# A routed-expert kernel: routing weights by tangent, one scan per chunk, the eight-largest instructions in small chunks, and filling rows in the first batch

## The chip, the cores and the metric

The kernel runs on one core of a Trainium2 chip. The metric is the device time of one execution in microseconds (us). The runs shown for the kernel before are 1497.51, 1497.18 and 1500.99 us, with a median of 1497.51. A profiled execution was recorded beside them. Of the engines, PE multiplies matrices, DVE works on vectors, ACT evaluates activation functions, POOL does general work and issues indirect DMAs (gathers and scatters by row numbers), and SP issues the plain DMAs. Each engine works through its own instructions in their order and waits on semaphores for the others.

## The reference, cut to what matters

The input x has 64 graphs ("batches") of 256 nodes with 256 features. Two layers follow one another; each is an attention over the graph's edges and then a feed-forward part, both added to x:

```python
x = x + gnn0(layernorm(x), adj)          # 4 heads, softmax over neighbours, elu
x = x + layernorm(x) @ weight.T + bias
x = x + gnn1(layernorm(x), adj)          # 1 head, softmax over neighbours, relu
x = x + moe(layernorm(x))                # below
```

The last part sends each row ("token") to two of eight experts:

```python
logits = tokens @ router_w.T
probs = softmax(logits)
rw, re = top_k(probs, 2)
rw = rw / max(rw.sum(-1), 1e-12)
combine = zeros(N, 8).at[row, re].set(rw)
out = tokens
for e in range(8):
    h = gelu(tokens @ w1[e] + b1[e])
    out = out + combine[:, e] * (h @ w2[e] + b2[e])
```

With the two largest logits a >= b, the two weights of a row depend on b - a alone: the first is 1 / (1 + exp(b - a)), the second 1 minus the first. Their difference is tanh((a - b) / 2).

## The kernel before, in words

**Batches and steps.** The program is written out by a loop in Python, which runs in steps; three steps (TICKS) begin one batch. In every step the active jobs (generators) are advanced in the order of their ranks, so each engine's order of instructions is fixed when the program is built. The job of a batch (`batch_layers`) does both attentions and the first feed-forward part on 256 rows, with everything in fp32. The inverse root for the norms runs on POOL (L408, L409, L446, L449, tile `rstd`), and at the end of the program on DVE. A batch ends with its normalized rows (`xng`), its logits (`lg`) and the rows `base` = x + layernorm(x), which SP stores into the output (L736).

**Chunks and routing.** CHUNKS is `(4,) * 11 + (2,) * 7 + (1,) * 3`: the first 61 batches are routed in 21 chunks of four, two or one batches. With NT = 2 tiles of 128 rows for each batch, a chunk has nt = 8, 4 or 2 tiles. `route` finds the two largest logits and their experts (`top_two`, L785 to L808), counts rows for each expert by two matmuls against ones (L1105, L1106), turns the counts into row places by a running sum over the tiles, expert by expert (L1116 in one instruction where nt is 8, otherwise one for each expert, L1122), takes the exponential of b - a on ACT (L1112), makes the two weights of it on DVE (`two_weights`, L812 to L815), and sends each row, with its own number and the two weights, to the region of each of its experts in a DRAM buffer `xs` (POOL's indirect DMAs, L1061). `allot` decides which pairs of tiles (256 rows of one expert) are full.

**Expert pairs.** `expert_pair` loads one pair (`xr`, L893) and its small columns (`xt`, L904) and the expert's first matrix (`we`, L922) on SP, multiplies twice on PE (`ph` L955, then `py` L970) with a Gelu on ACT between (`hT`, L961), adds the bias on DVE (`y`, L980), scales on ACT (L948), and puts the result into a list, from which one pair is taken in each step. `scatter` then adds the pair's 256 rows to the output by two indirect DMAs on POOL with addition (L991). Since two pairs may hold the same row, each pair's adds wait for the two adds before them:

```python
before = added[-2:] + based
```

**Filling rows.** A pair that isn't full at the end is filled with rows of the tile `fill`: zeros, weight 0, and as row number a row of the last batch, 63. They are added like all others, and add zero. So the last batch's rows are set to zero in setup (`fill_spare`, a 256 KB store on SP), and the last batch's own rows may be stored only when every add has landed.

**Dense batches.** The last three batches aren't routed. `route_dense` makes a weight for each row and expert (with an exponential, L1195, and `two_weights`), and `dense_expert` runs all eight experts on all their rows, adding into `base` on DVE (L1023). `store_dense` stores `base` on SP (L1036). For the last batch it holds the store back and then waits for the last adds:

```python
while b == B - 1 and (scatters or len(added) < 2 * PAIRS):
    yield 99
```

**Activation tables.** [...] the build puts a load (ACT_TABLE_LOAD) ahead of an activation whose function isn't in the set that is active. The kernel uses Exp (L479, L513, L647, L1112, L1195), Gelu (L961), and Square, Relu, Copy and Identity.

Of the kernel before, what the change touches and what calls it, by code (L numbers as in the profile page):

```python
# [15 lines left out]
P = 128  # L16
# [11 lines left out]
def kernel(  # L28
# [251 lines left out]
    def pack_expert(e):  # L280
# [22 lines left out]
    fill = const.tile([P, 2, ROW], F32, tag="fill", name="fill")  # L303
    nc.gpsimd.memset(fill, 0.0)
    nc.gpsimd.iota(
        fill[:, :, D : D + 1].bitcast(I32), pattern=[[1, 2], [1, 1]], base=(B - 1) * N,
        channel_multiplier=2,
    )
    nc.vector.memset(fill[:, :, D + 1 : D + 2], -1.0)
# [3 lines left out]
    def fill_spare():  # L313
        nc.sync.dma_start(
            out=xs_d[E * CAP * PAIR :, :].rearrange("(p t) c -> p t c", t=2), in_=fill
        )
        d = nc.sync.dma_start(
            out=out_rows[(B - 1) * N :, :].rearrange("(p t) c -> p t c", t=2), in_=fill[:, :, :D]
        )
        tc.add_to_no_dep_group("out", d.ins)  # L320
        based.append(d.ins)
        yield 90

    def once(work):
# [27 lines left out]
    em8 = iota([E], [[1, E]], -E, 0, "em8")  # L352
    jrow = iota([JOBS], [[1, JOBS]], 0, 0, "jrow")
    region = iota([E], [[CAP, E]], 0, 0, "region")
    scan_mask = const.tile([P, E, NTC], F32, tag="scan_mask", name="scan_mask")
    nc.vector.memset(scan_mask, 1.0)
    nc.vector.memset(scan_mask[:, :, 0:1], 0.0)

# [414 lines left out]
    def chunk_tile(shape, name, c, bufs=2, dt=F32):  # L773
        return keep.tile([P] + shape, dt, tag=name, name=f"{name}_{c}", bufs=bufs)
# [8 lines left out]
    def top_two(c, nt, lg, first):  # L783


        rt = lambda shape, name: chunk_tile(shape, name, c)
        vec, tt = nc.vector, nc.vector.tensor_tensor
        emb = em8[:, None, :].to_broadcast([P, nt, E])
        ohs, tops, lcur = rt([2, nt, E], "ohs"), [], lg
        for k in range(2):  # L790
            top = rt([nt], f"top{k}")
            vec.tensor_reduce(top, lcur, AX.X, ALU.max)
            eq = rt([nt, E], "eq")
            tt(eq, lcur, top[:, :, None].to_broadcast([P, nt, E]), ALU.is_equal)
# [12 lines left out]
        tt(ed, tops[1], tops[0], ALU.subtract)  # L807
        yield ohs, ed  # L808

    def two_weights(less, second, ed):  # L810

        nc.vector.tensor_scalar(less, ed, 1.0, None, op0=ALU.add)  # L812
        nc.vector.reciprocal(less, less)
        nc.vector.tensor_tensor(second, ed, less, ALU.mult)
        nc.vector.tensor_tensor(less, less, second, ALU.subtract)  # L815

    rows = [keep.tile([P, E], F32, tag="rows", name="rows")]  # L820
    nc.vector.tensor_scalar(rows[0], region, float(PAIR), None, op0=ALU.mult)
# [208 lines left out]
    def store_dense(b):  # L1030

        own = dense_batch[b]
        yield 99
        while b == B - 1 and (scatters or len(added) < 2 * PAIRS):
            yield 99
        d = nc.sync.dma_start(  # L1036
            out=out_rows[b * N : (b + 1) * N, :].rearrange("(t p) d -> p t d", p=P),
            in_=own["base"],
        )
        before = added[-2:] + based if b == B - 1 else []  # L1040
        tc.declare_no_dep(
            d.ins, query=SYNC, group="out", keep=before,
            reason="no row is added to here, or every add is in their chain",
        )
        for ins in before:
            tc.add_manual_dep(d.ins, ins.name, AFTER, reason="filling rows were added here")
        tc.add_to_no_dep_group("out", d.ins)
        nc.sync.nop()

# [29 lines left out]
    def route(c, row0, nt, n, last, xng, lg):  # L1079
# [32 lines left out]
        nc.scalar.activation(ed, ed, AF.Exp)  # L1112
        tt(tot[:, :, 0], tot[:, :, 0], rows[0], ALU.add)
        run = rt([E, nt], "run")
        if nt == NTC:
            vec.tensor_tensor_scan(  # L1116
                run.rearrange("p e t -> p (e t)"), scan_mask.rearrange("p e t -> p (e t)"),
                tot.rearrange("p e t -> p (e t)"), 0.0, ALU.mult, ALU.add,
            )
        else:  # L1120
            for e in range(E):
                vec.tensor_tensor_scan(  # L1122
                    run[:, e, :], ones[:, :nt], tot[:, e, :], 0.0, ALU.mult, ALU.add
                )
        rows[0] = run[:, :, nt - 1]
        tt(pre, pre, run, ALU.add)
        if spread:
# [8 lines left out]
        vec.tensor_copy(pos, posf)  # L1136
        if not spread:
            yield from later(90, 1, 2)
        two_weights(tail[:, :, 1], tail[:, :, 2], ed)
        for i, xe in enumerate(xng):  # L1140
            vec.tensor_copy(xe[:, :, D + 1 :], tail[:, i * NT : (i + 1) * NT, :])
        parts = allot(c, n, False)
# [47 lines left out]
    def route_dense(b, lg):  # L1190
# [4 lines left out]
        nc.scalar.activation(ed, ed, AF.Exp)  # L1195
        two = chunk_tile([2, NT], "two", c)
        two_weights(two[:, 0], two[:, 1], ed)
        nc.vector.tensor_tensor(two[:, 0], two[:, 0], two[:, 1], ALU.add)
        w = chunk_tile([NT, E], "wd", c, DENSE)
        nc.vector.tensor_tensor(  # L1200
# [8 lines left out]
                )  # L1209

    FLUSH = 2 * (E - 1)
    PAIRS = ROUTED * NT + E - 1

    def jobs():
        b = done = taken = 0
# [104 lines left out]
```

## Time and profile before

| | |
|---|---|
| median of three runs | 1497.51 us (1497.18 to 1500.99) |
| profiled execution, its own time | 1509.41 us |
| span, first to last instruction | 1507.6 us |
| mean granted PE clock | 0.986 |
| instructions | 30029 |
| table loads on ACT: in front of L961, L513, L1112, L647, L1195, L235 | 65, 47, 8, 6, 3, 1; 1283 ns each |
| indirect DMAs: adds into the output (L991), sends to the regions (L1061) | 258 and 244 |

The profile is one execution on the chip. "Busy" is the time in which an engine works on an instruction, as a share of the span. "Idle before, releaser" is the time that an engine waited ahead of an instruction, and whose semaphore came last. In the table by stage a row gives the stretch, its length, the busy time (and count) of PE, PEld (the loading of PE's weights), DVE, ACT and POOL, the granted PE clock, the share of DMA engines that were busy and GB/s. The profiled execution is 0.8% longer than the median of the runs, and its time is 1.8 us more than its span.

### The profile page before, as it was taken

The numbers are of one execution on the slowest core, as the hardware profiler recorded it, in microseconds if no ns is written. First come the engines' busy times: TensorE is split into PE (matmuls) and PEld (weight loads), VectorE is DVE, ScalarE is ACT, GpSimd is POOL, SyncE is SP. The second block draws the span as 40 slices with busy tenths as digits, with TensorE's granted clock in tenths as the row PEclk, the third lists the DMA queues.
The fourth block names the chain that finished last, engine by engine and source line by source line (L and its number), as shares of the span: only waits on it lengthen the run. The fifth ranks groups of instructions, "written<-read, shape, count | busy, mean of one in ns | idle before, by whom it ended". The sixth has DMA issues, their size and how long they took to land. (4 is left out here: it accounts for less than half of the span.)

```text
span 1507.6 us, 30029 instructions
## 1 busy us (share of the span) xinstructions
PE 1429.0 (95%) x8138; PEld 1263.9 (84%) x8138; DVE 1252.7 (83%) x4476; ACT 1024.6 (68%) x2403; POOL 870.2 (58%) x845
## 2 busy tenths in 40 slices
PE   6899999999999999999999999999999999879996
PEld 5788888889898998988998989888888887658885
DVE  7699999888898888889898988998888888765543
ACT  1477667577777777777777787667777878764331
POOL 2122536355867576666758585776666667643444
PEclk9899999899999999999999999999999999999999
DMA  4732334556877777877877677768777775887843
GB/s 134 241 97 67 117 104 131 155 149 142 196 172 190 157 183 155 177 177 180 187 157 183 151 186 164 181 164 187 179 167 170 153 170 124 192 180 161 156 83 50
DMA packets 354354, 236.37 MB, mean 157 GB/s; under 512 B 246276, under 2 KB 316428, under 8 KB 354188
## 3 DMA queue, kind: packets, MB, share of 16 engines
q1 hardware_dynamic: 301272, 158.16, 41.3%
q0 software_dynamic: 48864, 66.33, 23.8%
q10 hardware_dynamic: 4052, 9.98, 2.2%
q8 instruction: 67, 1.10, 0.3%
q14 instruction: 99, 0.81, 0.2%
HBM read 146.00 MB, written 88.35 MB: 155 GB/s over the span
## 5 line engine op out<-in xcount | busy, mean ns | idle before, releaser
L991 POOL DMA_INDIRECT out_dram<-y,xt x258 | 414.1, 1605 | 206.6 <-issue 71.5
L586 PE MATMUL pv<-q,z 128*128 128x65 f32 (+1 forms) x2560 | 365.9, 298 | 0.4
L586 PEld LDWEIGHTS pv<-q,z 128*128 128x128 f32 x2560 | 333.0, 194 | 13.1 <-DVE z L572 1.1
L1061 POOL DMA_INDIRECT xs<-xng,pos x244 | 259.5, 1064 | 65.3 <-issue 60.3
L970 PE MATMUL py<-w2s,hT 128*128 (+1 forms) x1224 | 283.5, 382 | 11.5 <-ACT hT L961 10.3
L970 PEld LDWEIGHTS py<-w2s,hT 128*128 128x128 f32 x1224 | 229.1, 191 | 45.4 <-ACT hT L961 14.2
L955 PE MATMUL ph<-sT,we 128*128 128x256 f32 x1032 | 241.9, 383 | 4.5 <-DVE y L980 2.9
L572 DVE SCALAR_TENSOR_TENSOR z<-z,q,mask 128x256 f32<-128x256 f32 x504 | 231.6, 482 | 15.5 <-DMA z<-terms 6.6
L955 PEld LDWEIGHTS ph<-sT,we 128*128 128x128 f32 x1032 | 195.6, 192 | 32.4 <-DVE y L980 3.6
L461 ACT COPY xT<-pt 128x512 f32<-128x512 f32 x209 | 121.4, 588 | 105.0 <-PE pt L455 72.2
L948 ACT ACTIVATE y<-y,w 128x256 f32<-128x256 f32 x258 | 113.2, 498 | 115.3 <-DVE y L980 100.9
L961 ACT ACTIVATE hT<-ph,we 128x256 f32<-128x256 f32 x306 | 124.1, 472 | 63.5 <-PE ph L955 46.3
L408 POOL TENSOR_SCALAR rstd<-mv 128x4 f32<-128x4 f32 (+1 forms) x66 | 15.6, 236 | 239.4 <-DVE mv L381 184.4
L506 PE MATMUL pq<-wx,xT 128*128 128x259 f32 x512 | 128.8, 394 | 18.6 <-ACT xT L461 16.9
L426 ACT ACTIVATE off<-x,sums 128x256 f32<-128x256 f32 x256 | 129.3, 505 | 8.4 <-DVE x L669 1.6
L506 PEld LDWEIGHTS pq<-wx,xT 128*128 128x128 f32 x512 | 95.6, 193 | 42.6 <-ACT xT L461 25.6
L471 PE MATMUL pq<-wx,xT 128*128 128x268 f32 x512 | 127.1, 391 | 2.8 <-DVE xT L117 1.6
L980 DVE TENSOR_TENSOR y<-py,b2s 128x512 f32<-128x512 f32 x129 | 85.7, 685 | 50.0 <-PE py L970 37.3
L662 PE MATMUL pf<-wfT,xT 128*128 128x256 f32 x512 | 123.8, 385 | 0.0
L471 PEld LDWEIGHTS pq<-wx,xT 128*128 128x128 f32 x512 | 97.5, 191 | 21.9 <-DVE xT L117 1.8
L690 ACT ACTIVATE rel<-pv,rinv 128x256 f32<-128x256 f32 x128 | 54.0, 469 | 76.4 <-DVE rinv L593 52.2
L662 PEld LDWEIGHTS pf<-wfT,xT 128*128 128x128 f32 x512 | 94.7, 195 | 10.8
(174 smaller groups left out, 2400.8 us busy)
## 6 DMA issues: line engine op xcount, KB each, us to landing
we<-wpack SPq DMA_DIRECT2D x145, 288.0 KB
xr<-xs SPq DMA_DIRECT2D x516, 64.0 KB
z<-terms SPq DMA_DIRECT2D x46, 512.0 KB
xin<-in_x_dram SPq DMA_DIRECT2D x64, 256.0 KB
out_dram<-base SPq DMA_DIRECT2D x61, 256.0 KB
xblk<-in_x_dram SPq DMA_DIRECT2D x188, 64.0 KB
z<-terms ACTq DMA_DIRECT2D x17, 512.0 KB
out_dram<-y,xt POOLq DMA_INDIRECT x258
```

Of the source, the lines that this page charges most:

```text
L426: nc.scalar.activation(off, src[:, t, :], AF.Square, bias=sums[:, t : t + 1], scale=-float(D), accum_out=sq[:, at + t : at + t + 1],)
L461: nc.scalar.copy(dst, pt)
L471: nc.tensor.matmul(pq.rearrange("p h c -> p (h c)"), xT[:, k, t * P : (t + 1) * P], wx[:, k, :], start=(k == 0), stop=(k == KT - 1),)
L506: nc.tensor.matmul(pq, xT[:, k, t * P : (t + 1) * P], wx1[:, k, :], start=(k == 0), stop=(k == KT - 1),)
L572: nc.vector.scalar_tensor_tensor(z[:, j, :, h, :], terms, q[:, j, h, HD + 2 : HD + 3], masks[0][:, j, :].rearrange("p (t i) -> p t i", t=N ...
L586: nc.tensor.matmul(pv[:, h, :], z(j, h, t), q[:, j, h, : d + 1], start=(j == 0), stop=(j == NT - 1),)
L662: nc.tensor.matmul(pf[:, t, :], xT[:, k, t * P : (t + 1) * P], wfT[:, k, :], start=(k == 0), stop=(k == KT - 1),)
L955: nc.tensor.matmul(ph[:, f, :], we[:, k * D + f * P : k * D + (f + 1) * P], xT[:, k, :], start=(k == 0), stop=(k == KT - 1),)
L961: nc.scalar.activation(hT[:, f, :], ph[:, f, :], AF.Gelu, bias=we[:, C_B1 + f : C_B1 + f + 1])
L970: nc.tensor.matmul(py[:, t, :], hT[:, f, t * P : (t + 1) * P], w2s[:, e, f * D : (f + 1) * D].rearrange("p e c -> p (e c)"), start=(f == 0 ...
L991: d = nc.gpsimd.indirect_dma_start(out=out_rows, out_offset=bass.IndirectOffsetOnAxis(ap=xt[:, t, 0:1].bitcast(I32), axis=0), in_=y[:, t, ...
L1061: d = nc.gpsimd.indirect_dma_start(out=xs_d[: E * CAP * PAIR, :], out_offset=bass.IndirectOffsetOnAxis(ap=at, axis=0), in_=xe, in_offset=None,
```

## The change

Five things are different.

1. The two weights come from tanh((a - b) / 2) instead of an exponential. The tangent is the row's weight column "less" itself (first minus second), and the second weight is 0.5 - 0.5 x tangent, one DVE instruction in place of four. This holds for routed and dense batches.
2. The running sum is one instruction in all chunks. For this there are three masks (nt = 8, 4, 2), set by six memsets on POOL in setup instead of two on DVE.
3. Where nt is 2 (the last three chunks and the dense batches) `top_two_of_few` takes the eight largest of the eight logits of a tile, sorted, and their positions, by two instructions for each tile.
4. Filling rows carry the numbers of rows of the first batch. The last batch's rows aren't set to zero in setup.
5. The last batch's store waits for no add and is begun when its sums are ready.

Apart from these, the order of instructions on each engine is the same. The built program has 116 table loads: 58 ahead of the Gelu, 47 ahead of L513's Exp, 10 ahead of the Exp of `e` (L647 before) and one in setup.

```diff
     nc.gpsimd.iota(
-        fill[:, :, D : D + 1].bitcast(I32), pattern=[[1, 2], [1, 1]], base=(B - 1) * N,
+        fill[:, :, D : D + 1].bitcast(I32), pattern=[[1, 2], [1, 1]], base=0,
         channel_multiplier=2,
     )
...
-        d = nc.sync.dma_start(
-            out=out_rows[(B - 1) * N :, :].rearrange("(p t) c -> p t c", t=2), in_=fill[:, :, :D]
-        )
-        tc.add_to_no_dep_group("out", d.ins)
-        based.append(d.ins)
         yield 90
...
-    scan_mask = const.tile([P, E, NTC], F32, tag="scan_mask", name="scan_mask")
-    nc.vector.memset(scan_mask, 1.0)
-    nc.vector.memset(scan_mask[:, :, 0:1], 0.0)
+    scan_masks = {}
+    for nt in sorted({nb * NT for nb in CHUNKS}):
+        m = const.tile([P, E, nt], F32, tag=f"scan_mask{nt}", name=f"scan_mask{nt}")
+        nc.gpsimd.memset(m, 1.0)
+        nc.gpsimd.memset(m[:, :, 0:1], 0.0)
+        scan_masks[nt] = m
...
+        if nt == NT:
+            yield top_two_of_few(c, nt, lg, first)
+            return
...
-    def two_weights(less, second, ed):
-
-        nc.vector.tensor_scalar(less, ed, 1.0, None, op0=ALU.add)
-        nc.vector.reciprocal(less, less)
-        nc.vector.tensor_tensor(second, ed, less, ALU.mult)
-        nc.vector.tensor_tensor(less, less, second, ALU.subtract)
+    def top_two_of_few(c, nt, lg, first):
+
+        top = chunk_tile([nt, E], "eq", c)
+        at = chunk_tile([nt, E], "l2", c, dt=mybir.dt.uint32)
+        for t in range(nt):
+            nc.vector.max(top[:, t, :], lg[:, t, :])
+            nc.vector.max_index(at[:, t, :], top[:, t, :], lg[:, t, :])
+        ohs = chunk_tile([2, nt, E], "ohs", c)
+        for k in range(2):
+            nc.vector.tensor_tensor(
+                ohs[:, k], jrow[:, None, :E].to_broadcast([P, nt, E]),
+                at[:, :, k : k + 1].to_broadcast([P, nt, E]), ALU.is_equal,
+            )
+        nc.vector.tensor_scalar(first, at[:, :, 0], float(-E), None, op0=ALU.add)
+        ed = chunk_tile([nt], "ed", c)
+        nc.vector.tensor_tensor(ed, top[:, :, 1], top[:, :, 0], ALU.subtract)
+        return ohs, ed
+
+    def second_weight(second, less):
+
+        nc.vector.tensor_scalar(second, less, -0.5, 0.5, op0=ALU.mult, op1=ALU.add)
...
         yield 99
-        while b == B - 1 and (scatters or len(added) < 2 * PAIRS):
-            yield 99
         d = nc.sync.dma_start(
             out=out_rows[b * N : (b + 1) * N, :].rearrange("(t p) d -> p t d", p=P),
             in_=own["base"],
         )
-        before = added[-2:] + based if b == B - 1 else []
...
-        nc.scalar.activation(ed, ed, AF.Exp)
+        nc.scalar.activation(tail[:, :, 1], ed, AF.Tanh, scale=-0.5)
         tt(tot[:, :, 0], tot[:, :, 0], rows[0], ALU.add)
         run = rt([E, nt], "run")
-        if nt == NTC:
-            vec.tensor_tensor_scan(
-                run.rearrange("p e t -> p (e t)"), scan_mask.rearrange("p e t -> p (e t)"),
-                tot.rearrange("p e t -> p (e t)"), 0.0, ALU.mult, ALU.add,
-            )
-        else:
-            for e in range(E):
-                vec.tensor_tensor_scan(
-                    run[:, e, :], ones[:, :nt], tot[:, e, :], 0.0, ALU.mult, ALU.add
-                )
+        vec.tensor_tensor_scan(
+            run.rearrange("p e t -> p (e t)"), scan_masks[nt].rearrange("p e t -> p (e t)"),
+            tot.rearrange("p e t -> p (e t)"), 0.0, ALU.mult, ALU.add,
+        )
...
-        two_weights(tail[:, :, 1], tail[:, :, 2], ed)
+        second_weight(tail[:, :, 2], tail[:, :, 1])
...
-        nc.scalar.activation(ed, ed, AF.Exp)
         two = chunk_tile([2, NT], "two", c)
-        two_weights(two[:, 0], two[:, 1], ed)
+        nc.scalar.activation(two[:, 0], ed, AF.Tanh, scale=-0.5)
+        second_weight(two[:, 1], two[:, 0])
```

More of the change, by code (lines that the diff above doesn't have):

```diff
@@ L1039, in store_dense @@
         )
-        before = added[-2:] + based if b == B - 1 else []
-        tc.declare_no_dep(
-            d.ins, query=SYNC, group="out", keep=before,
-            reason="no row is added to here, or every add is in their chain",
-        )
-        for ins in before:
-            tc.add_manual_dep(d.ins, ins.name, AFTER, reason="filling rows were added here")
+        tc.declare_no_dep(d.ins, query=SYNC, group="out", reason="no row is added to here")
         tc.add_to_no_dep_group("out", d.ins)
@@ L1111, in route @@
         pre, tot = both[:, 0], both[:, 1]
-        nc.scalar.activation(ed, ed, AF.Exp)
+        nc.scalar.activation(tail[:, :, 1], ed, AF.Tanh, scale=-0.5)
         tt(tot[:, :, 0], tot[:, :, 0], rows[0], ALU.add)
         run = rt([E, nt], "run")
-        if nt == NTC:
-            vec.tensor_tensor_scan(
-                run.rearrange("p e t -> p (e t)"), scan_mask.rearrange("p e t -> p (e t)"),
-                tot.rearrange("p e t -> p (e t)"), 0.0, ALU.mult, ALU.add,
-            )
-        else:
-            for e in range(E):
-                vec.tensor_tensor_scan(
-                    run[:, e, :], ones[:, :nt], tot[:, e, :], 0.0, ALU.mult, ALU.add
-                )
+        vec.tensor_tensor_scan(
+            run.rearrange("p e t -> p (e t)"), scan_masks[nt].rearrange("p e t -> p (e t)"),
+            tot.rearrange("p e t -> p (e t)"), 0.0, ALU.mult, ALU.add,
+        )
         rows[0] = run[:, :, nt - 1]
@@ L1211 @@
     FLUSH = 2 * (E - 1)
-    PAIRS = ROUTED * NT + E - 1
     def jobs():
```

## The prediction

> **What bounds the kernel now.** I read the page's totals first, then the chain that ended last, then POOL's own rows in order of time, because the chain ends on POOL.
>
> ```profile
> PE 1429.0 (95%) x8138; PEld 1263.9 (84%) x8138; DVE 1252.7 (83%) x4476; ACT 1024.6 (68%) x2403; POOL 870.2 (58%) x845
> PE   6899999999999999999999999999999999879996
> ```
>
> PE is nearly full, with a thin place in slices 35 and 36 (1281 to 1357 us) and at both ends. The stage table gives sizes (stretch, length, then PE busy):
>
> ```profile
> 100.00:940.00 840.00, 825.63 (x4931) 741.66 (x4931) 749.01 (x2609) 618.96 (x1498) 513.11 (x508) 0.99 0.66 157
> 1280.00:1320.00 40.00, 32.67 (x144) 26.64 (x143) 30.16 (x172) 29.00 (x61) 25.81 (x23) 0.91 0.86 188
> 1320.00:1350.00 30.00, 22.27 (x104) 17.32 (x102) 22.33 (x103) 18.89 (x39) 14.34 (x13) 1.00 0.83 180
> 1350.00:1400.00 50.00, 48.14 (x222) 42.06 (x223) 27.14 (x74) 22.27 (x50) 20.02 (x13) 1.00 0.81 160
> ```
>
> The chain view walks back through PE from 1496 to 1351 us, but its last steps are POOL's last add into the output:
>
> ```profile
> 1495.80 0.47 ACT hT L961
> 1496.27 0.37 ACTq L1315
> 1496.64 1.22 issue
> 1497.86 1.56 POOL out_dram L991
> 1499.42 1.86 POOLq L1315
> ```
>
> POOL's rows in order of time show that those adds are a chain of their own:
>
> ```profile
> 1478.09 1.56 POOL L991 DMA_INDIRECT out_dram<-y,xt  x1 [3.04 <-DMA out_dram<-y,xt]
> 1479.95 1.56 POOL L991 DMA_INDIRECT out_dram<-y,xt  x1 [0.30 <-issue]
> 1484.51 1.56 POOL L991 DMA_INDIRECT out_dram<-y,xt  x1 [3.00 <-DMA out_dram<-y,xt]
> 1486.37 1.56 POOL L991 DMA_INDIRECT out_dram<-y,xt  x1 [0.30 <-issue]
> ```
>
> Each pair's two adds wait for the landing of the pair before and start some 0.75 us after it (1.5 at most). From 1310 us on, 27 pairs follow one another so. The last y is scaled at 1476.7 us and added at 1497.86: data come some 20 us early. The period is 6.4 us after the last expert pair and 7.3 us on average before. So from about 1300 us two chains run side by side: PE's (last matmul 1498.3) and the adds' (last landing 1503.6). Then SP, which held the last batch's store for that landing, issues it (1503.73); it lands at 1505.87, and POOL's closing drain ends at 1506.83.
>
> ```profile
> SPq L1036 <- DMA out_dram<-y,xt: 7.2, 1, 7.2
> ```
>
> [...] no second part is seen (the load of 1230.31 ends at 1231.59, the activation starts at 1231.61), so 1.283 us is used. [...] The program as built puts no load at any tangent, beside exp or gelu. [...] the last add's issue ends at 1501.28 and it lands at 1503.58, 2.3 us.
>
> **The change part by part.**
>
> *Tangent, ACT.* Loads now:
>
> ```profile
> L1112 ACT ACT_TABLE_LOAD x8 | 10.3, 1283 | 0.1
> L1195 ACT ACT_TABLE_LOAD x3 | 3.8, 1283 | 0.1
> ```
>
> Those 11 go, with 7 that brought gelu back (L961), and 4 come at e (L647): the built program has 116 for 130. 14 x 1.283 = 18.0 us of ACT. All seven pairs saved lie after 1230 us (four chunks of two or one batch, three dense batches). The four moved ones belong to the chunks at 1038, 1089, 1138 and 1187 us. At 1038 nothing stood between load and e. At 1089, 1138 and 1187 ACT sat idle 1.14 to 1.44 us behind the load, waiting for y, so it was free; now it comes after that y, ahead of e, the squares, hT and the next xT. PE took that xT 1.6 and 1.5 us after it was there at 1146 and 1195 us: covered. At 1097.38 PE was already waiting for it: a loss of 1.3 us.
>
> *Weights, DVE.* 24 times three instructions fewer: 11 x (205 + 172 + 173) ns + 7 x (180 + 166 + 166) + 6 x some 490 = 12.6 us.
>
> *Scan.* Ten chunks do eight scans of 2 or 4 elements; the eight take 0.72 us to the next instruction (1190.17 to 1190.88). One scan over 64 elements takes 316 ns, one over 4 157: over 32 I estimate 230, over 16 190. Saved: some 0.46 us x 10 = 4.6 us.
>
> *Eight largest.* Six times (three chunks, three dense batches) 12 instructions in 2.25 us (1272.71 to 1274.96) become 8: two largest, two indices, two comparisons, two small ones. Low end: 0.16 us each, as the reductions of that size, 1.2 us in all[...]. I take 1.7: 0.55 x 6 = 3.3 us saved[...].
>
> DVE is thus relieved of some 20 us of 1252.7. Most of it lies behind PE.
>
> *Six memsets on POOL for two on DVE.* They follow the q memsets at 8.9 us, some 0.1 us each; POOL then idles 4.24 us before rstd at 13.48. Nothing; without that gap 0.6 us.
>
> *Filling rows.* One 256 KB store fewer on SP in setup: nothing, PE there waits for x and xT. The adds of the filling rows keep their number. The last store loses its wait; behind it on SP stands only the end.
>
> The path, stage by stage:
> 1. To 940 us PE idles 14.4 us of 840. Eleven chunks give DVE 0.55 us each: I take 1.0 (0 to 3).
> 2. 940 to 1207: PE waited for DVE's y at 1049.9, 1150.5 and 1199.8 us (1.47, 1.07 and 0.35 us), behind runs of back-to-back DVE work that hold the scans: 0.45 + 0.45 + 0.35, some 1.2; the weights, which stand before sT and the statistics, 0.6; the moved load -1.3. Sum 0.5 (-1.3 to 3).
> 3. 1207 to 1300: POOL leads. It waits for compute at 1207.44 (1.38 us, DVE's statistics, behind a DVE run with a scan: 0.45) and 1272.41 (1.09 us, squares behind an exp load that stays). The load at 1233.44 held y for 1.28 us, but POOL was busy until 1234.89, so 0.14. Sum 0.6 (0 to 2.5).
> 4. 1300 to the end: PE's waits at 1328.0 (0.79), 1330.8 (2.43), 1348.0 (3.32) and 1372.4 (0.50) hang on the dense batches' loads: tangent 1.28 sooner, three DVE instructions fewer, no gelu load. Some 6 us close. What is late next is the add chain, which does not look at PE. It gains only because loads end 6 us sooner: 6 x (1 - 6.4 / 7.3) = 0.7 (-2 to 3).
> 5. The end: SP is through at 1506.24; without the store, at about 1504.0: 2.2. POOL's drain ended 0.6 us after SP, 3.2 after the last add landed and 5.5 after its issue ended, and no row says what it waits for: 0 if on the adds, 2.2 if on quiet DMA. I take 2.2, with both ends kept.
>
> Sum 1.0 + 0.5 + 0.6 + 0.7 + 2.2 = 5.0 us from the profiled execution: its span 1507.6 to 1502.6, its time 1509.4 to 1504.4. The median of the runs shown, 1497.5, is 0.8% below the profiled time; 5.0 us (0.33%) from it give 1492.5.
>
> **The rivals.**
> *A: the add chain holds everything.* For: it is unbroken from 1310, and POOL's drain may hang on the adds. Then stages 3 to 5 give nothing and 1.5 us remain: 1496.0.
> *B: PE's chain is the bound, as the chain view has it.* For: PE is busy without a break from 1373 to 1477. Then the 6 us of stage 4 count whole, 5.0 - 0.7 + 6 = 10.3: 1487.2. Against: data wait 20 us for the adds.
> *C: slower, by the moved loads.* ACT's 1.283 us now stands ahead of e and the next xT in four chunks. All four on PE's path, and nothing won: 4 x 1.28 = 5.1 more, 1502.6. It decides once xT's slack (1.6 and 1.5 us) falls below 1.28, which an earlier PE or later y brings about; one of four is there now. Against: stages 1 and 2 win as much.
> That the change doesn't do what it says is left out: loads, scans and weights are gone from the built program.
>
> **How the numbers follow.** 0.3% (4.5 us) is about what a measurement of this kernel can tell from no change. Forecast 0.43 (1489.5 to 1495.5 of its own, mid-way over the line: 0.26 faster, 0.17 same), A 0.23 (0.02 faster, 0.20 same, 0.01 slower), B 0.23 (0.22, 0.01, 0), C 0.11 (0, 0.01, 0.10). Sums: faster 0.50, same 0.39, slower 0.11. The range leaves out B's faster half and most of C: 1485.5 to 1499.5[...].
>
> **What would show it.** Right: 116 loads, none at routing; PE's waits of 1328 to 1351 us mostly gone, so PE's last matmul some 8 us sooner while the last add moves 3 or less; that add 0.75 us behind the landing before it; the last store issued before the last add; POOL's drain ending within a microsecond of 1504.5. Wrong, if PE's last matmul and the last add move together (B), if the drain still ends 3.2 us after the last landing (step 5), if PE waits for xT behind a load at e in more than one chunk (C), or if one of the new instructions takes over 0.5 us.

## The result and the profile after

The changed kernel takes 1489.54 us (median of six, 1487.59 to 1490.35) where the kernel before takes 1497.35 (median of six, 1496.77 to 1503.31). The ratio is 0.9936, with a 95% interval of 0.9918 to 0.9954: by the medians 7.8 us less, by the ratio 9.6 us (6.9 to 12.3). The forecast was 1492.5 us, between 1485.5 and 1499.5. The changed kernel's own profiled execution took 1489.83 us, with a span of 1488.0.

The two traces differ by more than the kernels do. The profiled execution of before, from which I predicted, takes 7 us longer between 420 and 910 us than a second trace of the same kernel (below), and 7 us longer between 260 and 420, so the 19.6 us between the two spans don't measure the change. Of the first 7 us PE idles 3.9, most of it waiting for xT; for the rest I found no reason in the rows. Where an "earlier" or "later" is given below, it is against that second trace, whose span is 1492.9 us.

The totals and PE's slices of the changed kernel's page:

```profile
PE 1420.1 (95%) x8138; PEld 1264.0 (85%) x8138; DVE 1232.9 (83%) x4320; ACT 1006.5 (68%) x2389; POOL 864.6 (58%) x851
PE   6899999999999999999999999999999999899994
```

DVE has lost 19.8 us (forecast some 20), ACT 18.1 (forecast 18.0). The thin place of PE's slices 35 and 36 has closed up to one 8, and the last slice has become thinner: PE is done earlier. The table by stage (stretch, length, busy time of PE, PEld, DVE, ACT and POOL, granted clock, DMA share, GB/s) shows the same:

```profile
100.00:940.00 840.00, 832.81 (x5025) 753.11 (x5024) 758.12 (x2635) 631.08 (x1527) 511.73 (x517) 1.00 0.67 160
1280.00:1320.00 40.00, 35.90 (x169) 29.81 (x168) 31.99 (x164) 25.84 (x62) 23.63 (x21) 0.96 0.92 221
1320.00:1350.00 30.00, 30.00 (x141) 26.41 (x140) 17.60 (x51) 12.63 (x31) 13.11 (x10) 1.00 0.87 170
1350.00:1400.00 50.00, 50.00 (x233) 44.03 (x232) 25.40 (x57) 18.28 (x43) 20.25 (x14) 1.00 0.79 158
```

PE's idle time of 7.7 us between 1320 and 1350 is gone. The chain that ended last no longer walks through PE at the end; it consists of the adds and their landings (start, length, what):

```profile
1465.88 4.32 DMA out_dram<-y,xt
...
1472.97 3.83 DMA out_dram<-y,xt
...
1476.92 1.42 issue
1478.34 1.56 POOL out_dram L1004
1479.89 1.86 POOLq L1313
```

POOL's rows in order of time, the number in brackets being the idle time ahead of each:

```profile
1471.03 1.63 POOL L1004 DMA_INDIRECT out_dram<-y,xt  x1 [3.60 <-DMA out_dram<-y,xt]
1472.97 1.56 POOL L1004 DMA_INDIRECT out_dram<-y,xt  x1 [0.30 <-issue]
1478.34 1.56 POOL L1004 DMA_INDIRECT out_dram<-y,xt  x1 [3.81 <-issue]
1480.20 1.56 POOL L1004 DMA_INDIRECT out_dram<-y,xt  x1 [0.30 <-issue]
```

PE's last matmul ends at 1469.28 us and the last pair's y is scaled at 1447.27, 31 us before it is added (some 20 us in the first trace of before). Against the second trace of before, PE's last matmul is 18.3 us earlier (1487.59 to 1469.28) and the last pair's adds 4.4 us (1482.72 to 1478.34). The prediction's sign was 8 us and 3 or less; both moved further, since this trace is 6.0 us earlier already at the last batch's Exp of `e` (1258.1 and 1252.1 us). The last pair starts 1.54 us behind the landing ahead of it (1476.80), where the sign was 0.75. The last add lands at 1483.97, and POOL's drain, which starts at 1478.57 and takes 8.636 us, ends at 1487.21, 3.24 us after that landing (in the view of the line: shortest, median and longest in ns, first and last start):

```profile
L1313 POOLq DRAIN  x3: 46/113/8636, 1478.6 to 1487.8; - x3
```

The last batch's store, in order of time and in SP's view of waits (us in total, times, longest), waits for its sums and for no add, and SP then stands at the end until the adds are through. It is issued at 1471.26 us, before the last adds:

```profile
1471.26 0.39 SPq L1047 DMA_DIRECT2D out_dram<-dbase  x1
```

```profile
SPq L1047 <- DVE dbase L1036: 46.0, 2, 42.1
SPq L1313 <- DMA out_dram<-y,xt: 12.3, 1, 12.3
```

The table loads on ACT, in the view by line (busy us, mean ns, idle before), are the 116 of the built program, and none stands at a tangent:

```profile
L974 ACT ACT_TABLE_LOAD x58 | 74.4, 1283 | 1.0
L511 ACT ACT_TABLE_LOAD x47 | 60.3, 1283 | 0.8
L645 ACT ACT_TABLE_LOAD x10 | 12.8, 1283 | 0.1
L235 ACT ACT_TABLE_LOAD x1 | 1.3, 1283 | 1.8 <-issue 1.8
```

In ACT's rows of the first trace of before, 64 loads of the 130 stand where an Exp follows a Gelu, 65 where a Gelu follows an Exp, and one in setup. In the changed kernel's, of the 24 tangents 13 follow an Exp and 11 a Gelu, all without a load, and the Gelu that follows a tangent (7 times) has none either.

The new DVE instructions, in the view by line and shape:

```profile
L817 DVE FIND_INDEX8 l<-eq,lg 128x8 uint32<-128x8 f32 x12 | 1.9, 160 | 0.0
L816 DVE MAX8 eq<-lg 128x8 f32<-128x8 f32 x12 | 1.8, 154 | 0.0
L1120 DVE TENSOR_TENSOR_SCAN run<-scan_mask,both 128x32 f32<-128x32 f32 x7 | 1.6, 224 | 0.2
L817 DVE MATCH_VALUE_LOAD l<-eq,lg 128x8 f32 x12 | 1.1, 92 | 0.4
```

The scans take what was estimated (224 ns for 230, and 191 for 190 over 16 elements). The eight-largest are at their low end: from the first MAX8 at 1235.73 us to the instruction behind the group at 1236.85 there are 1.12 us, where 2.25 stood before and 1.7 were taken.

### The profile page after: what moved, and what is told of

Read it like the earlier page. It is cut to its first block, busy times and chain, and to the rows that moved or that the text cites. A ratio compares the mean times of both kernels' runs of the same rounds, so it can differ in the third digit from the quotient of the medians.

```text
span 1488.0 us, 29865 instructions
## 1 busy us (share of the span) xinstructions
PE 1420.1 (95%) x8138; PEld 1264.0 (85%) x8138; DVE 1232.9 (83%) x4320; ACT 1006.5 (68%) x2389; POOL 864.6 (58%) x851
## 5 line engine op out<-in xcount | busy, mean ns | idle before, releaser
L1066 POOL DMA_INDIRECT xs<-xng,pos x244 | 256.3, 1050 | 65.2 <-issue 57.7
L504 PEld LDWEIGHTS pq<-wx,xT 128*128 128x128 f32 x512 | 96.0, 192 | 33.6 <-ACT xT L459 19.8
```

What stands on the lines that cost most here:

```text
L504: nc.tensor.matmul(pq, xT[:, k, t * P : (t + 1) * P], wx1[:, k, :], start=(k == 0), stop=(k == KT - 1),)
L1066: d = nc.gpsimd.indirect_dma_start(out=xs_d[: E * CAP * PAIR, :], out_offset=bass.IndirectOffsetOnAxis(ap=at, axis=0), in_=xe, in_offset=None,
```

## The experiments

The theories: F, the forecast (PE hides most of the relief up to 1300 us, and from there the chain of adds holds the end); A, the adds hold everything; B, PE's chain is the bound; E, the gain is made by DVE's relief before 940 us. Microseconds are worked out as (ratio - 1) times the median of before measured beside that kernel. All kernels except e8 compute the whole.

A caution for all of them: single times of one kernel lie far apart (before beside e5 to e8: 1493.0 to 1504.24). The gains of 9.6 (the change), 8.2 (e2) and 5.7 us (e4) come from six or seven times each; e3, e6, e9 and e12 have 22 each and give 1.8, 4.8, 6.0 and 2.7.

For the stages I use marks that every trace has: the start of the Exp of `e` of a batch (L647, L645), counted from batch 0. From batch 8 to 24 is some 140 to 416 us, to 48 some 896, to 63 some 1255. The lengths, in us (traces where DVE waits for PE at `rinv` are marked *, explained at e1; e9 to e11, marked too, follow below):

| kernel | weights in the four-batch chunks | 8 to 16 | 16 to 24 | 24 to 48 | 48 to 63 | 63 to the last pair's adds |
|---|---|---|---|---|---|---|
| before, first trace * | exponential | 122.9 | 158.7 | 487.5 | 360.4 | 228.6 |
| before, second trace (e1) | exponential | 121.5 | 151.7 | 480.4 | 362.3 | 224.7 |
| e7, filling rows | exponential | 121.4 | 155.1 | 480.3 | 359.5 | 231.7 |
| e3, tangent late | exponential | 121.5 | 155.1 | 480.3 | 359.3 | 224.1 |
| e4, old weights | exponential | 121.5 | 151.8 | 480.3 | 358.2 | 225.1 |
| e6, early exponential | exponential | 122.5 | 155.2 | 480.3 | 356.0 | 227.7 |
| e5, three more | exponential and 3 | 125.0 | 156.4 | 481.5 | 357.2 | 227.5 |
| e2, tangent early | tangent | 120.2 | 151.0 | 480.3 | 357.4 | 225.0 |
| after | tangent | 120.2 | 152.8 | 480.4 | 355.8 | 226.2 |
| e8, two fewer | tangent | 120.1 | 152.8 | 480.4 | 359.0 | (two pairs fewer) |
| after, second trace (e12) * | tangent | 120.2 | 158.6 | 487.0 | 361.9 | 228.3 |

### e1: the kernel before once more

No edit.

> The kernel before, unchanged, for a second trace and for the size of no change. Forecast's view: the trace of before was an ordinary execution apart from its span; a second trace again shows PE waiting for xT at L506 some 13 times between 300 and 900 us, 5.8 us in all (before 5.8, changed kernel 0.0), and the last add starts 1495 to 1500 us. Rival (the early lead belongs to that one execution): the second trace has less than half of these waits, and its last add starts before 1490 us. Time: a ratio of 1.000 within 0.3%.

Measured: ratio 0.9997 (0.9986 to 1.0008). The waits weren't there again. The first trace's view of waits, 420 to 900 us (us in total, times, longest), has for PE and DVE:

```profile
PE pq L506 <- ACT xT L461: 3.2, 5, 0.8
```

```profile
DVE rinv L593 <- PE pt L455: 10.2, 12, 1.2
```

(At `rinv` a further 1.7 us are put down to another releaser.) The second trace has neither row in that stretch: PE is busy all the time there, in the table by stage

```profile
420.00:900.00 480.00, 480.00 (x2856) 1.00 0.76 176
```

and in the first trace it isn't, with 50 PE instructions fewer done:

```profile
420.00:900.00 480.00, 476.13 (x2806) 1.00 0.76 174
```

So the wait at `rinv` is the mark of such an execution. Of the fourteen traces five have it (12 to 20 us in this stretch), nine don't have it at all, and it stands in kernels of both kinds. The first trace of before was one of the five. The other four were taken where before, measured beside them, took 1507 or 1511 us, and the nine without it where before took 1496 to 1498. So the first trace's delay at xT between 420 and 900 us, which the changed kernel's trace lacks, is not something that the change removed.

### e2 and e3: the tangent alone, early and late

```diff
+        if spread:            # e2: the eleven four-batch chunks; e3: "not spread", and the dense batches
+            nc.scalar.activation(tail[:, :, 1], ed, AF.Tanh, scale=-0.5)
+        else:
+            nc.scalar.activation(ed, ed, AF.Exp)
...
+        if spread:
+            second_weight(tail[:, :, 2], tail[:, :, 1])
+        else:
+            two_weights(tail[:, :, 1], tail[:, :, 2], ed)
```

> Before with the tangent's weights in the eleven four-batch chunks alone: 11 x 3 DVE instructions of some 183 ns fewer between 157 and 932 us, no table load moved or saved, all else as before. Forecast (step 1): 1.0 us at most 3 by 940 us, of which the end keeps little: -0.5 to -1.5 us. Rival E (DVE's delay in these chunks is what stalls PE at xT, L506): the waits of 300 to 900 us go, 7 us or more of lead by 940 us, and the measured gain is most of the 7.8 us: -5 to -8 us. Rival A (the adds hold everything from 1310 us): whatever lead is there at 1056 us reaches the end, since the adds are paced from there; it allows 1.0 or 7 alike.

> Before with the tangent's weights in the seven two-batch, three one-batch chunks and the three dense batches alone: 14 table loads fewer on ACT (116 for 130), 13 x 3 DVE instructions fewer, all after 940 us. Forecast (steps 2 to 4): 0.6 of weights less 1.3 at the moved load, 0.14, and 0.7 of the 6 us that PE closes: -0.2 us, PE's last matmul 5 to 6 us sooner. B (PE's chain is the bound): -5 to -6 us. E: within 1 us of before, since the gain is made before 940 us.

Measured, e2: 1486.55 us, ratio 0.9945 (0.9927 to 0.9964), 8.2 us less (5.4 to 10.9). e3: 1493.53 us, ratio 0.9988 (0.9976 to 1.0), 1.8 us less (0 to 3.6).

e3 tests F against B. PE's two longest waits for a Gelu behind the dense batches' loads, in the second trace of before (in order of time):

```profile
1320.77 2.40 PE L970 MATMUL py<-w2s,hT 128*128 x8 [2.43 <-ACT hT L961]
...
1339.06 1.47 PE L970 MATMUL py<-w2s,hT 128*128 128x256 f32 x3 [3.32 <-ACT hT L961]
```

are gone in e3, and PE's last matmul ends 9.7 us earlier (1487.59 to 1477.93); the last pair's adds start only 2.3 us earlier (1482.72 to 1480.42). By B they would have moved together. F's small gain holds; its 0.2 us lie inside the interval. One thing in the second trace of before qualifies this: there the two chains end almost together. Its chain that ended last closes with

```profile
1485.60 2.01 PE py L970 x8
...
1489.07 0.48 DVE dbase L1023
```

Behind these sums stands the last batch's store, which keeps SP until 1492.09 us, while the drain behind the adds ends at 1491.83. So before's end can hang on either chain, and once the PE chain is shortened the adds alone hold it. e3 also shows the loss at the moved load alone. The same matmul in the second trace of before and in e3:

```profile
1087.95 2.02 PE L506 MATMUL pq<-wx,xT 128*128 128x259 f32 x8 [0.34 <-ACT xT L461]
```

```profile
1088.50 1.80 PE L506 MATMUL pq<-wx,xT 128*128 128x259 f32 x7 [1.76 <-ACT xT L461]
```

That is 1.4 us for a forecast of 1.3, at the one of the four places that was forecast. The other three cost nothing that PE's waits show.

e2 gains about as much as the whole change, which step 1 excluded. The number is the one that E gave, but not for E's reason: PE's waits for xT, which by E should go, aren't there in e1 either, and from batch 24 to 48 e2 and e1 take 480.3 and 480.4 us. Part of the gain is in the table: 1.3 us from batch 8 to 16 and 0.7 from 16 to 24, against e1. The rest of the 8.2 us has no place that the traces show. e2's trace is also 5 us shorter than e1's from batch 48 to 63, where the two kernels have the same instructions, and so are e5's and e7's by 3 to 5.

### e4: all the rest without the tangent

```diff
-        nc.scalar.activation(tail[:, :, 1], ed, AF.Tanh, scale=-0.5)
+        nc.scalar.activation(ed, ed, AF.Exp)
...
-        second_weight(tail[:, :, 2], tail[:, :, 1])
+        two_weights(tail[:, :, 1], tail[:, :, 2], ed)
```

> The changed kernel with the exponential's weights put back everywhere (130 table loads, four DVE instructions for the weights): what is left is the single scans, the eight-largest instructions, the memsets and the filling rows. Forecast: scans 1.2 us before 1207 us and 0.9 to 1300, the eight-largest behind the adds, and 2.2 at the end if the drain waits for quiet DMA: -2.1 to -4.3 us. E: nothing before 940 us, the xT waits of 300 to 900 us are there again, and the drain counts from the adds as the changed kernel's trace has it: 0 to -2 us. In every theory the weights' part is 7.8 us less this.

Measured: 1488.12 us, ratio 0.9962 (0.994 to 0.9984), 5.7 us less (2.4 to 9.0): more than any theory gave. F's upper end of 4.3 is inside the interval, but 2.2 of it is the drain's part, which e7 puts at nothing. With e2 and e3 the parts sum to 15.7 us, where the whole measured 9.6. The parts overlap a little: PE's waits at the experts' first matmul (`ph`, L955) between 940 and 1200 us are 0.78, 0.82, 0.89 and 0.37 us in e1, 2.9 in all. e3, with the tangent, keeps 0.39, 0.78, 0.57 and 0.27, and e4, with the single scans, 0.60, 0.34 and 0.15; the changed kernel keeps 0.32 and 0.17. That is 0.9 and 1.8 us for the parts and 2.4 for the whole, so this overlap accounts for some 0.3 us of the 6 that the parts sum to beyond the whole. The rest is not shown; the intervals of the four ratios are wide enough for most of it.

### e5 and e6: the early weights, more and less

```diff
+        if spread:            # e5, on before, behind the weights; ed isn't read again
+            for _ in range(3):
+                vec.tensor_scalar(ed, ed, 1.0, None, op0=ALU.add)
```

e6 is the changed kernel with the exponential and the four instructions in the four-batch chunks (the edit of e4 under `if spread`).

> Before with three more DVE instructions of some 0.18 us behind the weights of each four-batch chunk (0.55 us a chunk, 6 us in all; they write a tile that nothing reads any more): the opposite dose of what the change takes away there. Step 1 as forecast (PE covers DVE there): +1.0 us, at most +3. Edge theory (PE, ACT and DVE run there so close to one another that some executions make PE wait for xT at L506 in every chunk and others in none; the first trace of before held 5.8 us of it between 300 and 900 us, the second 1.1 at the start): more DVE work brings the waits into every execution, +4 to +9 us, and some 0.5 to 0.8 us of wait per chunk between 300 and 900 us in the trace.

> The changed kernel with the exponential's weights put back in the eleven four-batch chunks alone. Step 1 as forecast: 1.0 us slower than the changed kernel, so some -6.5 us from before. Edge theory: it loses what the tangent alone won in those chunks, up to 8 us in the executions that wait: a median between -1 and -6 us from before and a spread of single times that reaches over 6 us, where the changed kernel's six times lie within 2.8.

Measured, e5: 1501.33 us, ratio 1.0015 (0.9997 to 1.0032), 2.2 us more (-0.4 to 4.8). e6: 1494.58 us, ratio 0.9968 (0.9955 to 0.9981), 4.8 us less (2.8 to 6.7), and single times from 1487.81 to 1499.96.

Against the changed kernel's first ratio, e6 puts some 4.8 us on the early weights, not 1.0; but against its second (e12, 2.7 us) it puts nothing on them, so the times alone don't settle it. The traces show where the early weights act. In batches 12 and 16 PE waits for `ex` of ACT, behind DVE's run that holds the chunk's weights. PE's rows in e5 (three instructions more), in the second trace of before, and in e2 (three fewer):

```profile
225.38 0.32 PE L525 MATMUL pd<-ident,ex 128*128 128x128 f32 x1 [0.86 <-ACT ex L513]
...
292.48 0.99 PE L525 MATMUL pd<-ident,ex 128*128 128x128 f32 x2 [2.51 <-ACT ex L513]
```

```profile
224.57 0.32 PE L525 MATMUL pd<-ident,ex 128*128 128x128 f32 x1 [0.49 <-ACT ex L513]
...
288.31 0.32 PE L525 MATMUL pd<-ident,ex 128*128 128x128 f32 x1 [1.95 <-ACT ex L513]
```

```profile
221.58 0.32 PE L525 MATMUL pd<-ident,ex 128*128 128x128 f32 x1
...
284.67 0.32 PE L525 MATMUL pd<-ident,ex 128*128 128x128 f32 x1 [1.31 <-ACT ex L513]
```

Each step of 0.55 us of DVE moves these two waits by some 0.4 to 0.6 us. The table has the sum: from batch 8 to 16, 120.1 or 120.2 us in all four listed traces with the tangent, 121.4 to 122.9 in all six with the exponential, 125.0 with three more; e9 and e10 (120.2 and 120.1) and e11 (122.9) fall in with them. From 24 to 48 the traces without the mark take 480.3 to 481.5 us with any dose: there PE hides DVE, as step 1 said.

Not all of these differences are the waits themselves. In some traces PE's granted clock stands at half (0.50) for 3.41 to 10.24 us behind such a wait (more at e9), and those are the longer ones. From 8 to 16, the traces with the exponential and no such stretch take 121.4 or 121.5 us, those with one of 3.41 us 122.5 or 122.9, and e5, with one of 3.41 and one of 6.83, 125.0. From 16 to 24, unmarked, it is 151.0 (tangent) and 151.7 or 151.8 (exponential) without a stretch, 152.8 with 6.83 us of it, and 155.1 or 155.2 with 10.24 (e5, with two of them, 156.4). So without any stretch the early weights are worth 1.3 + 0.7 = 2.0 us.

The edge theory, that more DVE work brings the waits for xT into every execution, is refuted by e5: PE has 0.4 us of them between 300 and 900 us, where the first trace of before had 5.8. e6's time and its spread of 12 us are what that theory expected, but e6's trace has none of these waits, and before beside it spreads over 11 us as well.

### e7: the filling rows alone

```diff
-        d = nc.sync.dma_start(
-            out=out_rows[(B - 1) * N :, :].rearrange("(p t) c -> p t c", t=2), in_=fill[:, :, :D]
-        )
...
-        while b == B - 1 and (scatters or len(added) < 2 * PAIRS):
-            yield 99
```

and the base of the row numbers 0.

> Before with the filling rows alone: rows of the first batch, no store of zeros in setup, no wait of the last batch's store. Step 5 as forecast (the drain waits for quiet DMA): -2.2 us, the drain ending some 0.6 us after SP is through. Step 5 refuted (the drain counts from the adds): 0.0 us at the end, the drain ending 3.2 us after the last add has landed though the last store was issued earlier. The setup store counts nothing in either.

Measured: ratio 0.9994 (0.9976 to 1.0011), 0.9 us less (-1.6 to 3.6). Its last pair, POOL's rows in order of time:

```profile
1488.20 1.55 POOL L986 DMA_INDIRECT out_dram<-y,xt  x1 [4.25 <-issue]
1490.06 1.56 POOL L986 DMA_INDIRECT out_dram<-y,xt  x1 [0.30 <-issue]
```

The second add's issue ends at 1491.62 us, it lands at 1493.87, and the drain ends at 1497.11, 3.24 us after the landing. In the second trace of before, where the last batch's store lands at 1491.71, the drain ends at 1491.83, again 3.24 us after the last add's landing (1488.59). With and without a store at the end the drain keeps its distance to the adds: it doesn't wait for quiet DMA. The drain of e7, in the view of its line:

```profile
L1302 POOLq DRAIN  x3: 46/113/8677, 1488.4 to 1497.7; - x3
```

### e8: two pairs fewer to add

```diff
-        for t in range(2):
+        for t in range(2 if len(added) < 2 * 127 else 0):
             d = nc.gpsimd.indirect_dma_start(
```

> The changed kernel without the adds into the output of its last two pairs (their rows are left out; the matrix work and the scaling of these pairs stay). Forecast and A (the chain of adds sets the end): two periods of 6.4 us less than the changed kernel, -12 to -13 us, so some -20 us from before. B (PE's chain is the bound): the changed kernel's time within 1 us, -7 to -8 us from before.

Measured: 1478.84 us, ratio 0.9857 (0.9831 to 0.9883), 21.4 us less than before (17.5 to 25.3), so 11.8 below the changed kernel's ratio. PE's work is whole, and its last matmul ends at 1471.51 us, 2.2 later than in the changed kernel's trace. The last adds, in order of time:

```profile
1468.53 1.56 POOL L1004 DMA_INDIRECT out_dram<-y,xt  x1 [3.07 <-DMA out_dram<-y,xt]
1470.39 1.56 POOL L1004 DMA_INDIRECT out_dram<-y,xt  x1 [0.30 <-issue]
```

What the end moves by is near two periods of the chain (12.8 us). With PE's work whole, this refutes B for the changed kernel from the other side, too.

### e9 to e11: PE kept busy in its waits

PE's granted clock stands at half (0.50) in places. In the first traces of the two kernels the half-speed stretches ahead of the program's end are 3.41, 6.83 or 10.24 us long, to within the last digit. One follows the wait at 285 us in eight of the eleven traces without these edits, of kernels of both kinds, 6.83 us in the changed kernel's first trace and 10.24 in its second. Three traces (e1, e2, e4) have the wait and no stretch. That the wait brings the stretch on was my guess, and no trace shows how. So I filled waits with work that changes nothing:

```diff
+    def busy(out, n):
+        for _ in range(n):
+            nc.tensor.transpose(out, ident, ident)
...
         pd = bank("pd", [N])
+        busy(pd[:, :P], {16: 11}.get(b, 0))
```

e10 has further such lines ahead of seven other waits; e11 is before with 17 transposes at that place.

> The changed kernel with eleven further transposes of the identity (some 0.11 us each by the rows of pt, 1.2 us in all) on PE ahead of the one wait at 285.8 us (L523, 1.31 us, batch 16), written into the bank that the next transposes overwrite: PE works where it stood still, nothing else moves. Clock theory (TensorE's half-speed stretch of 289 to 296 us follows that wait; in the traces such stretches are multiples of 3.41 us, the changed kernel's 6.83, before's 10.24): clock 1.00 from 285 to 300 us, 2 to 4 us earlier by 416 us than the changed kernel in its trace, and the time 1 to 3 us below its own (ratio to before some 0.991). Without it[...]: the half-speed stretch stays, the time within 1 us of the changed kernel's.

> The changed kernel with such transposes ahead of its eight longest waits of PE (batch 16 at L523; batches 50, 51, 54, 55 and 62 at L504; two transposes of batches at L453, 1221.8 and 1266.1 us), each set a little shorter than its wait. Clock theory: no half-speed stretch between 85 and 1350 us where the changed kernel has 17 us of them (some 8.5 us of PE's time), of which what lies before 1260 us, some 5 us, reaches the adds: 2 to 5 us below the changed kernel. Without it, or if the adds are held by their own landings from before 1056 us: within 1 us of it; over 1 us slower if the transposes delay what they stand in front of.

> Before with seventeen such transposes ahead of its wait at 285.4 us (L525, 1.95 us, batch 16), nothing of the change. Clock theory: the stretch of 10.24 us at half speed, which three of the four traces with before's weights in the four-batch chunks show there, is gone: 2 to 4 us below before, and the single times lie closer together. Without it: within 1 us of before.

The "four traces" of the last text are those of kernels built from before; of all six with the exponential in those chunks, four have the stretch.

Measured against before at 1511.22 us: e9 0.996 (0.9947 to 0.9974), e10 0.9978 (0.9958 to 0.9998), e11 0.9994 (0.9979 to 1.0008). The clock did what was expected. The row of 290 to 295 us (PE busy, granted clock, DMA share, GB/s) in the changed kernel and in e9:

```profile
290.00:295.00 5.00, 5.00 (x23) 0.50 0.68 111
```

```profile
290.00:295.00 5.00, 5.00 (x30) 1.00 1.00 233
```

In e9 and e11 the stretch is gone, and in e10 all of them between 85 and 1300 us, where the first traces of before and of the changed kernel have five and four. The mean granted clock is 0.985 in e9, 0.990 in e10 and 0.989 in e11 (before 0.986, the changed kernel 0.985). The time didn't follow: e11 is before's time within its interval, and e10 isn't faster than e9. All three traces have the waits at `rinv` (13 to 20 us from 420 to 900 us), and from batch 24 to 48 they take 488.9 to 491.1 us instead of 480.3, with PE waiting for xT for part of it; this may have taken the gain, which is not shown. In e11's trace it was PE's chain that set the end, not the adds. The last pair's adds and the end of the chain that ended last:

```profile
1494.47 1.56 POOL L996 DMA_INDIRECT out_dram<-y,xt  x1 [3.80 <-issue]
1496.33 1.80 POOL L996 DMA_INDIRECT out_dram<-y,xt  x1 [0.30 <-issue]
```

```profile
1501.38 2.01 PE py L975 x8
...
1504.84 0.48 DVE dbase L1028
```

POOL's drain ended at 1503.49 us, but the last batch's store, which needs these sums, was issued only at 1505.36, and SP was through at 1507.87. What the half-speed stretches cost in the end is therefore not settled, and no version better than the changed kernel came of it: e9's 0.996 is not below the changed kernel's first ratio of 0.9936, and lies below its second (e12); neither pair was measured side by side.

### e12: the changed kernel once more

No edit.

> The changed kernel, unchanged, for a second trace and a second ratio. Forecast, corrected (four us before 420 us, two to three between 900 and 1260, none at the end): a ratio of 0.994 to 0.996, the last add some 9 us behind PE's last matmul, the drain ending 3.2 us after the last landing. If the waits for xT between 420 and 910 us (7 us in the first trace of before, 8 to 11 in the three kernels with the further transposes, none in the eight others) belong to the changed timing of those kernels, they are absent here; if they come and go by chip or execution, they may be here too. Rival B: PE's last matmul and the last add less than 3 us apart.

Measured against before at 1506.69 us: 0.9982 (0.9966 to 0.9998), 2.7 us less (0.3 to 5.1). The trace has the waits at `rinv` (20.1 us from 420 to 900 us) and 487.0 us from batch 24 to 48, so these come with the execution and not with the transposes of e9 to e11. The last add is 10.7 us behind PE's last matmul, against B. The ratio is outside what I expected and its interval doesn't overlap the first one's: where before takes 1507 us instead of 1497, the change measured less. The two marked traces can be set side by side: from batch 8 to the last pair's adds e12 takes 2.1 us less than the first trace of before, with 2.7 of it from 8 to 16 and nothing clear behind. The two unmarked ones (after and e1) are 5.2 us apart. Why is open.

## Why the prediction was right, and where its sum was wrong

The time, 1489.5 us, is 3 us below the forecast, inside the range. The bound of the changed kernel was named rightly: e3 and e8 show that the chain of adds holds its end and that PE's chain doesn't, so that B, whose 1487.2 us lies even nearer to the result, is wrong as a mechanism. For the kernel before the two chains are closer than the prediction had them: by the second trace they end within 0.3 us. And steps of the sum were off in opposite directions, so that the closeness of the number is in part luck. (Means below are over the traces of the table without the mark *.)

- **The pieces.** 18.0 us of ACT and some 20 of DVE, the scans' 230 and 190 ns, 116 loads and none at a tangent: all as forecast. The eight-largest were over-priced, 1.7 us against 1.12: no row of before has these instructions, and the 1.7 was my estimate.
- **Step 1 (1.0 us, at most 3): mis-sized.** It measured 3.1: from batch 8 to 24 the five traces with the exponential take 275.5 us on average, the three with the tangent 272.4. Of this, 2.0 us is left when only traces without a half-speed stretch there are compared (e1 and e4 against e2); the rest is those stretches, and the prediction has no term for them. From 24 to 48 it is nothing. I had spread 14.4 us of idle PE over 840 us and concluded that 0.55 us of DVE would mostly be hidden. But 10.5 us of it stand in some fifteen waits before 420 us (3.9 more are those of that one execution, 420 to 900), and two of the waits hang on just that stretch of DVE's work, so that there the 0.55 us count nearly in full.
- **Steps 2 and 3 (0.5 + 0.6 us): mis-sized.** From batch 48 to 63 the traces without the late parts (e1, e2, e5, e7) take 359.1 us on average, those with all of them (after, e6, e8) 356.9: 2.2 us, with single traces 5 us apart, so this is a mean and no more. The single waits are surer for step 2. PE's waits at `ph` lost 2.4 us instead of the 1.2 and 0.6 that step 2 gives scans and weights, and the moved load cost 1.4 (e3) where it was expected: 1.0 us instead of 0.5.
- **Step 4 (PE closes 6, the adds gain 0.7): right in that PE's 6 us don't reach the end.** The waits of 2.43 and 3.32 us are gone, and from batch 63 to the last adds those same groups (without e8) take 227.2 and 227.0 us. Whether the adds gain 0.7 or nothing, traces of one kernel apart by several microseconds (224.1 to 231.7 in all) can't tell.
- **Step 5 (2.2 us): wrong.** Of its two ends I took the one where the drain waits for quiet DMA. In before, after and e7 it ends 3.24 us after the last add's landing, whatever SP does: 0.0 us. The prediction had named this as its sign of being wrong.
- **Sum.** 3.1 + 2.2 + 0.2 + 0 = 5.5 us where 5.0 were forecast: step 5's 2.2 too much hid the 3.2 that steps 1 to 3 had too little. The measurements of the whole lie on both sides, 9.6 us (6.9 to 12.3) and 2.7 (0.3 to 5.1).

Rival A gave stages 3 to 5 nothing: a lead from before the chain of adds reaches the end, and what happens beside the chain doesn't. In stages 4 and 5 the traces are nearer to A (0.2 and 0.0 us) than to the forecast (0.7 and 2.2), though A's 1496.0 us is farther from the result. C's mechanism acted at one place out of four and was outweighed.

What stays open: why e2 alone measures as much as the whole, what delays PE at `rinv` in five of the traces, and why the gain is smaller where before is slower. How the gain divides among the parts is not shown; the scans and the eight-largest were never taken apart.

## What to carry to other kernels

Idle time that is small as a share can still be all in a few waits; ask of each which engine's run it hangs on, and a relief of that run counts there nearly in full (here 0.4 to 0.6 us of wait for 0.55 us of DVE), however well it is hidden elsewhere. When two chains run side by side at the end, a test that moves one by a known amount (two adds fewer, six us of PE closed) tells which one holds, where the totals can't; in the kernel before, the two may still end together. And take a second trace of the kernel before: of the 19.6 us between two single executions here, 14.7 stood between two traces of the same kernel.

## What the runs showed of the hardware

- POOL's closing drain ends 3.24 us after the last indirect add has landed (in 13 of the 14 traces; 3.34 in e8), and 5.3 to 5.7 us after that add's issue has ended. In e11 it ends before the last store is even issued (1503.49 and 1505.36).
- A half-speed stretch (granted clock 0.50) near 290 us follows a wait of PE of 1.3 to 2.5 us in eight of eleven traces and is absent in all three where the wait was filled with transposes. The stage from batch 16 to 24 takes 1.8 us longer with 6.83 us of half speed (152.8 against 151.0) and 3.4 longer with 10.24 (155.2 against 151.8).
- MAX8 over 8 elements takes 154 ns, the value load 92, FIND_INDEX8 160, and two of each with their small followers 1.12 us.
- In the first trace of before, one of the five marked by `rinv`, PE's semaphore rises late there against PE's own records: `rinv` starts at 664.41 us behind a rise at 664.38, which the profile puts down to a matmul of `pt` that starts in its record at 662.96. In the changed kernel's first trace the semaphore rises 0.29 or 0.30 us after the start of the last matmul of `pt` in all 72 groups from 420 to 900 us. What holds PE there, no run shows.
